# Perceiver block on one core: rows of a context block, its staging and the keys padded to whole 64 bytes

## The chip, the cores and the metric

The kernel runs on one core of one Trainium2 chip. The metric is device time in microseconds (us), the median of several runs. A core has five engines that run side by side: TensorE (PE in the profile; its weight loads are PEld), VectorE (DVE), ScalarE (ACT), GpSimd (POOL) and SyncE (SP), whose queue issues all of this kernel's DMAs. Tiles lie in the on-chip memory SBUF, 128 partitions wide; a tile's row is what one partition holds of it.

## The reference

The input is x, 8 x 64 x 512, and a context of 8 x 1601 x 512. Two layers are computed: cross-attention to the context, a state-space block, a ternary linear map, a second cross-attention, a self-attention and an octonion-structured gated map. Only the first cross-attention touches the change:

```python
q = (query @ Wq + bq).reshape(B, L, NKV, G, HDIM)     # 8 x 64 queries, 32 heads of 128
k_, v_ = jnp.split(kv @ Wkv + bkv, 2, axis=-1)        # 1601 rows of context, 8 key heads
scores = jnp.einsum('blkgd,bmkd->bkglm', q, k) * scale
attn = jax.nn.softmax(scores, axis=-1)
o = jnp.einsum('bkglm,bmkd->blkgd', attn, v).reshape(B, L, NHEAD * HDIM)
return o @ Wo + bo
```

Keys and values have to be worked out for all 1601 rows of each of the 8 batches.

## The kernel before

Accuracy near fp32 is kept by splitting each operand into a high and a low half (type fp32r) and adding three products: high x high, high x low, low x high. The helper `split` (L96) makes the halves: ScalarE writes the high one (L101, or L104 with a bias), and another engine subtracts it from the source for the low one (L102 or L105).

The transposed context of one batch is taken in six blocks of columns, `BLK` (L27): five of 256 and a last one of 322, for 1601 rows padded to 1602. `x_ctx` (L291) loads a block in four pieces of 128 partitions into a staging tile `cst` (three buffers, L300), and splits each into the block's tile, GpSimd writing the low half. Blocks 0 to 4 use `cxb` (five buffers, L298), block 5 uses `cxt` (one buffer, L296). Either holds 2 halves x 4 pieces of rows in a partition; a row of `cxb` has 256 words, one of `cxt` 322, which is 1288 bytes.

Work goes over 64 units, (batch b, key head i), in `x_all` (L501 on). In a unit, six steps s run over the blocks:
- `x_k` (L345) makes the keys of a block: 12 matmuls (4 pieces x 3 products) with the weights wk as the stationary operand and the context as the moving one, into k_ps; then `split` with a bias writes both halves of the tile `kt` (three buffers, L356; rows of 322 words for every block, though five of the six fill 256).
- `x_v` (L310) makes the values of a tile of 128 context rows: 12 matmuls with the context stationary and the weights wv moving, into v_ps. Tiles 10 and 11 (and 12, of 65 rows) come out of `cxt`. It runs once for two heads.
- `x_s` (L360) makes scores: for each 128 keys three matmuls with kt stationary and the queries q moving, into s_ps, which ScalarE copies (L377) and VectorE takes a maximum of (L379, L381).
- softmax (`x_exp`, L405), values (`x_av`, L428) and the output weights (`x_wo`, L470) follow one unit later.

Beside this, generators of the other layers (`chain`, `prep`) are advanced by a planner's costs, so that their work fills gaps; the last group of two batches runs its chain alone in the last tenth of the time. `cxt`, `cxb`, `cst` and `kt` are in one pool, `xp`, whose tiles stand in memory in the order of their first use: S, wk, cxb, cst, kt, wv, q, mx, v, cxt, and then mc, ss, sl, rw, ot, wo. A tile's start is rounded up to 32 bytes.

Of the kernel before, what the change touches and what calls it, by code (L numbers as in the profile page):

```python
# [9 lines left out]
FR = mybir.dt.float32r  # L10
# [6 lines left out]
P = 128  # L17
D = 512
NC = 4
T = 64  # L20
LK = 1601
LP = 1602
NKV = 8
G = 4
NT = 13
# [50 lines left out]
class Kernel:  # L76
# [66 lines left out]
    def consts(self):  # L143
# [12 lines left out]
        def ld(name, shape):  # L156
            t = c.tile(shape, FP, name="c_" + name)
            nc.sync.dma_start(out=t, in_=i[name])
            return t

        self.bq = ld("bq", [P, 32])
        self.bk = ld("bk", [P, NKV])
        self.bv = ld("bv", [P, NKV])

# [24 lines left out]
    def scratch(self):  # L189
# [3 lines left out]
        def t(name, shape):  # L193
            return d.tile(shape, FP, name="d_" + name)

        B = self.B
        self.wk_s = [t(f"wk{k}", [P, 2, NC, P]) for k in range(NKV)]
        self.wv_s = [t(f"wv{k}", [P, 2, NC, 256]) for k in range(NKV // 2)]
        self.q_s = [t(f"q{k}", [B, P, 2, G, T]) for k in range(NKV)]
        self.wo_s = [t(f"wo{k}", [P, G, 2, D]) for k in range(NKV)]  # L200
        self.ot_s = [[t(f"ot{g}_{k}", [P, 1 + (g > 0), G, T]) for k in range(NKV)] for g in range(B // 2)]
# [89 lines left out]
    def x_ctx(self, b, k):  # L291

        nc = self.nc
        o, w = BLK[k]
        if k == 5:
            t = self.sb("cxt", [P, 2, NC, 322], FR, pool=self.xp, bufs=1)  # L296
        else:
            t = self.sb("cxb", [P, 2, NC, 256], FR, pool=self.xp, bufs=5)  # L298
        for c in range(NC):
            st = self.sb("cst", [P, 322], pool=self.xp, bufs=3)  # L300
            nc.sync.dma_start(out=st[:, :w], in_=self.i["ctxT"][b, c, :, o : o + w])
            self.split(t[:, 0, c, :], t[:, 1, c, :], st[:, :w], eng=nc.gpsimd)
        self.ctxb[(b, k)] = t
# [41 lines left out]
    def x_k(self, b, i, blk, w):  # L345

        nc = self.nc
        wd = BLK[blk][1]
        cx = self.cblk(b, blk)
        ps = self.px.tile([P, D], FP, name=self.nm("k_ps"), tag="kv", bufs=KVB)  # L350
        k = 0
        for c in range(NC):
            for a, m in ((0, 0), (0, 1), (1, 0)):
                nc.tensor.matmul(ps[:, :wd], lhsT=w[:, a, c, :], rhs=cx[:, m, c, :], start=k == 0, stop=k == 11)  # L354
                k += 1
        kt = self.sb("kt", [P, 2, 322], FR, pool=self.xp, bufs=3)  # L356
        self.split(kt[:, 0, :wd], kt[:, 1, :wd], ps[:, :wd], bias=self.bk[:, i : i + 1])
        return kt

# [616 lines left out]
    def xattn1(self, bs, x, xo):  # L976
# [7 lines left out]
        def scores(k, b):  # L984
            q0 = k * T
            if self.tail:
                s = self.sb("bc", [T, LP])
                S = [s[:, :512], s[:, 512:1024], s[:, 1024:]]
# [368 lines left out]
def _layout(inp):  # L1357
# [7 lines left out]
    r["ctxN"] = cx  # L1365
    ct = np.zeros((B, D, LP), f)
    ct[:, :, :LK] = np.transpose(cx, (0, 2, 1))
    r["ctxT"] = ct.reshape(B, NC, P, LP)
    r["Wq"] = inp["L0_xattn_Wq"].reshape(NC, P, NKV, D).transpose(2, 1, 0, 3)
# [66 lines left out]
```

## Time and profile before

| | |
|---|---|
| time, median of 3 runs | 2748.9 us (2741.76 to 2750.92) |
| the profiled execution | 2747.45 us, span 2745.6 us |
| TensorE busy | 2584.6 us, 94% of the span, 17840 matmul records |
| VectorE, ScalarE, GpSimd busy | 1756.7, 1378.4, 1163.1 us |
| v_ps matmuls from cxb, from cxt | 3840 (521.5 us), 1152 |
| k_ps matmuls from cxb, from cxt | 3840 (560.9 us), 768 (128.3 us) |
| s_ps matmuls | 2496 (414.9 us) |
| loads into cst | 192 DMAs |

Busy time of a group is the union of its instructions' spans. Matmuls are pipelined: the mean duration of one is longer than its distance to the next, so the distance between starts is worked out from the timeline where it matters. The chain of work that ended last is followed back from the last instruction; its shares say whose time set the end.

### The profile page before, as it was taken

To read this page: it belongs to the slowest core of one execution; us is meant where nothing else is said; L and a number is where in the kernel's file an instruction comes from. 1 tells how busy PE (TensorE), PEld (TensorE's weight loads), DVE (VectorE), ACT (ScalarE), POOL (GpSimd) and SP (SyncE) were. 2 spreads that over 40 slices of the span, in tenths; PEclk is the share of its full clock that TensorE was granted. 3 is DMA by queue.
4 is the path that set the end of the run, shared out by engine and by line. 5 is a ranking of instruction groups with operands and counts; after the bars stand their busy time and mean duration, and the time that the engine had idled before them with its cause. 6 is when DMAs were issued, how large, how long until landed. Compare 5 with 4: busy or idle time off the path is not lost.

```text
span 2745.6 us, 47783 instructions
## 1 busy us (share of the span) xinstructions
PE 2584.6 (94%) x17840; PEld 2303.7 (84%) x17840; DVE 1756.7 (64%) x2988; ACT 1378.4 (50%) x3318; POOL 1163.1 (42%) x1175
## 2 busy tenths in 40 slices
PE   7999999999999899999999989999999999976778
PEld 6999999889889899978988988988897998954545
DVE  4544345577777886545587787454668787549645
ACT  4444555444556554544456555444556555435433
POOL 3212444474579653421367344421348435215220
PEclk9999999999999999999999999999999999978889
DMA  9544446664666234664325534665333543465676
GB/s 305 151 144 152 131 155 221 204 205 156 212 208 212 71 116 164 215 192 155 114 78 156 156 106 131 199 203 165 125 101 97 168 153 126 146 221 197 219 253 218
DMA packets 312167, 460.03 MB, mean 168 GB/s; under 512 B 81272, under 2 KB 188792, under 8 KB 307456
## 3 DMA queue, kind: packets, MB, share of 16 engines
q1 hardware_dynamic: 311936, 456.99, 51.6%
q8 instruction: 140, 2.29, 0.3%
q14 instruction: 91, 0.75, 0.1%
HBM read 384.42 MB, written 72.48 MB: 166 GB/s over the span
## 4 chain that ended last, share of the span: by engine, by line
PE 60%; DVE 15%; DMA 9%; POOL 7%; issue 5%; ACT 4%; SPq 1%; POOLq 0%; DVEq 0%; ACTq 0%
PE v_ps L325 14%; PE k_ps L354 13%; PE o_ps L438 8%; PE s_ps L374 7%; DVE a L62 4%; PE w_ps L495 3%; POOL a L62 3%; PE acc L270 2%; POOL ss L426 2%; PE acc L1000 2%; PE acc L1053 2%; PE acc L740 2%; DMA cst<-in_ctxT_dram 2%; PE acc L743 1%; PE acc L785 1%
## 5 line engine op out<-in xcount | busy, mean ns | idle before, releaser
L354 PE MATMUL k_ps<-cxb,wk 128*128 128x256 f32 x3840 | 560.9, 291 | 21.8 <-ACT cxb L101 9.6
L354 PEld LDWEIGHTS k_ps<-cxb,wk 128*128 128x128 f32 x3840 | 504.9, 191 | 55.8 <-issue 15.1
L325 PE MATMUL v_ps<-wv,cxb 128*128 128x256 f32 x3840 | 521.5, 283 | 7.4 <-DVE mx L381 3.3
L325 PEld LDWEIGHTS v_ps<-wv,cxb 128*128 128x128 f32 x3840 | 479.2, 189 | 28.2 <-issue 13.9
L374 PE MATMUL s_ps<-q,kt 128*128 128x256 f32 (+1 forms) x2496 | 414.9, 299 | 13.3 <-DVE kt L105 4.9
L438 PE MATMUL o_ps<-S,v 128*128 128x256 f32 (+1 forms) x1664 | 409.2, 380 | 1.7 <-ACT S L416 1.6
L374 PEld LDWEIGHTS s_ps<-q,kt 128*128 128x128 f32 (+1 forms) x2496 | 339.7, 185 | 38.0 <-DVE kt L105 7.2
L381 DVE TENSOR_TENSOR mx<-s_ps,mx 128x512 f32<-128x512 f32 x256 | 175.3, 685 | 306.5 <-ACT S L377 306.3
L426 POOL TENSOR_TENSOR ss<-ss,S 128x512 f32<-128x512 f32 x256 | 355.0, 1387 | 16.2 <-ACT S L416 1.5
L377 ACT COPY S<-s_ps 128x512 f32<-128x512 f32 (+1 forms) x448 | 241.5, 551 | 211.8 <-PE s_ps L374 210.7
L438 PEld LDWEIGHTS o_ps<-S,v 128*128 128x128 f32 (+1 forms) x1664 | 296.4, 190 | 33.9 <-ACT S L416 2.5
L418 POOL TENSOR_TENSOR ss<-S,S 128x512 f32<-128x512 f32 x64 | 84.2, 1316 | 566.2 <-ACT S L416 566.0
L104 ACT ACTIVATE kt<-k_ps,c_bk 128x256 fp32r<-128x256 f32 (+1 forms) x384 | 184.7, 481 | 220.1 <-PE k_ps L354 216.1
L105 DVE SCALAR_TENSOR_TENSOR kt<-k_ps,c_bk,kt 128x256 fp32r<-128x256 f32 (+1 forms) x384 | 187.7, 489 | 144.0 <-ACT kt L104 143.2
L415 DVE TENSOR_TENSOR S<-S,m_ps 128x512 f32<-128x512 f32 (+1 forms) x448 | 257.6, 641 | 28.6 <-PE m_ps L401 27.6
L416 ACT ACTIVATE S<-S 128x512 f32<-128x512 f32 (+1 forms) x448 | 247.2, 599 | 42.5 <-DVE S L415 41.9
L328 ACT COPY v<-v_ps 128x256 f32<-128x256 f32 (+1 forms) x416 | 152.3, 367 | 219.6 <-PE v_ps L325 217.9
L62 ACT ACTIVATE a<-lv,c_A_log 128x128 f32<-128x128 f32 x384 | 122.7, 392 | 126.6 <-DVE lv L62 120.3
L62 POOL TENSOR_TENSOR a<-bc,lv 128x512 f32<-128x512 f32 x96 | 128.2, 1336 | 127.7 <-DVE a L62 112.4
L102 POOL TENSOR_TENSOR cxb<-cst,cxb 128x256 fp32r<-128x256 f32 x160 | 126.3, 804 | 120.9 <-ACT cxb L101 118.0
L62 DVE TENSOR_TENSOR_SCAN a<-a,a 128x512 f32<-128x512 f32 x96 | 145.1, 1512 | 48.3 <-POOL a L62 47.9
L325 PE MATMUL v_ps<-wv,cxt 128*128 128x256 f32 (+1 forms) x1152 | 161.8, 286 | 2.2 <-DVE kt L105 2.2
(348 smaller groups left out, 3972.0 us busy)
## 6 DMA issues: line engine op xcount, KB each, us to landing
wo<-d_wo SPq DMA_DIRECT2D x96, 512.0 KB, 4.9
wk<-d_wk SPq DMA_DIRECT2D x63, 512.0 KB, 3.4
wv<-d_wv SPq DMA_DIRECT2D x31, 1024.0 KB, 7.0
cst<-in_ctxT_dram SPq DMA_DIRECT2D x160, 128.0 KB, 3.1
b<-in_ctxN_dram SPq DMA_DIRECT2D x36, 512.0 KB, 4.2
d_q<-q_t SPq DMA_DIRECT2D x32, 512.0 KB, 4.3
q<-d_q SPq DMA_DIRECT2D x64, 256.0 KB, 3.6
d_wo<-b SPq DMA_DIRECT2D x32, 512.0 KB, 2.9
```

What stands on the lines that cost most here:

```text
L62: return lambda *a, **k: self.tc.keep_in_program_order(f(*a, **k))
L104: nc.scalar.activation(hi, src, AF.Identity, bias=bias)
L105: eng.scalar_tensor_tensor(lo, src, bias, hi.bitcast(FP), ALU.add, ALU.subtract)
L325: nc.tensor.matmul(ps[:r], lhsT=cx[:, a, c, o : o + r], rhs=w[:, m, c, :], start=k == 0, stop=k == 11)
L354: nc.tensor.matmul(ps[:, :wd], lhsT=w[:, a, c, :], rhs=cx[:, m, c, :], start=k == 0, stop=k == 11)
L374: nc.tensor.matmul(sp[:r, gi, :], lhsT=kt[:, a, u * P : u * P + r], rhs=q[:, m, :], start=k == 0, stop=k == 2)
L377: nc.scalar.copy(s[:r, :n], sp[:r, :n])
L381: nc.vector.tensor_tensor(mx, sp, S[0] if len(S) == 1 else mx, ALU.max)
L415: nc.vector.tensor_tensor(sv, sv, ps[:r, 1:2].to_broadcast([r, w, 256]), ALU.add)
L416: nc.scalar.activation(sv, sv, AF.Exp, scale=ISC)
L426: nc.gpsimd.tensor_tensor(ss, ss, S[n], ALU.add)
L438: nc.tensor.matmul(ps[:, 0], lhsT=self.v[(b, j, t)][:r, hc : hc + P], rhs=S[t // 2][:r, t % 2], start=t == 0, stop=t == NT - 1)
```

## The change

A constant KW = 336 replaces 322 as the row length of the three tiles, so that a row has 1344 bytes, 21 times 64, instead of 1288. The tile `cxt` is allocated with the longer rows and its first 322 columns are used; of `cst` and `kt` the same columns are used as before. The pool's tiles grow by 448 bytes (cxt), and, with the rounding, 3 x 32 (cst) and 3 x 96 (kt), 832 together.

In the two builds every engine's instructions stand in the same order. Addresses in SBUF (bytes in a partition):

| tile | before | after |
|---|---|---|
| cst | 97536, 98848, 100160 | 97536, 98880, 100224 |
| kt, low half 1288 or 1344 on | 101472, 104064, 106656 | 101568, 104256, 106944 |
| wv | 109248 | 109632 |
| q | 117440, 119488 | 117824, 119872 |
| cxt, row r at r x 1288 or 1344 | 139968 | 140352 |
| wk | 48384, 52480 | the same |
| cxb | 56576 to 89344, 8192 apart | the same |

Lines of the changed kernel stand 2 lower.

```diff
@@ -20,6 +20,8 @@
 LP = 1602
+
+KW = 336
 NKV = 8
@@ -293,11 +295,11 @@
         if k == 5:
-            t = self.sb("cxt", [P, 2, NC, 322], FR, pool=self.xp, bufs=1)
+            t = self.sb("cxt", [P, 2, NC, KW], FR, pool=self.xp, bufs=1)[:, :, :, :w]
         else:
             t = self.sb("cxb", [P, 2, NC, 256], FR, pool=self.xp, bufs=5)
         for c in range(NC):
-            st = self.sb("cst", [P, 322], pool=self.xp, bufs=3)
+            st = self.sb("cst", [P, KW], pool=self.xp, bufs=3)
@@ -353,7 +355,7 @@
-        kt = self.sb("kt", [P, 2, 322], FR, pool=self.xp, bufs=3)
+        kt = self.sb("kt", [P, 2, KW], FR, pool=self.xp, bufs=3)
```

## The prediction

> **What bounds the kernel now.** I read the page from the top: engine totals, slices, chain.
>
> ```profile
> span 2745.6 us, 47783 instructions
> PE 2584.6 (94%) x17840; PEld 2303.7 (84%) x17840; DVE 1756.7 (64%) x2988; ACT 1378.4 (50%) x3318; POOL 1163.1 (42%) x1175
> ...
> PE   7999999999999899999999989999999999976778
> ...
> PE 60%; DVE 15%; DMA 9%; POOL 7%; issue 5%; ACT 4%; SPq 1%; POOLq 0%; DVEq 0%; ACTq 0%
> PE v_ps L325 14%; PE k_ps L354 13%; PE o_ps L438 8%; PE s_ps L374 7%; DVE a L62 4%; PE w_ps L495 3%; POOL a L62 3%; PE acc L270 2%; POOL ss L426 2%; PE acc L1000 2%; PE acc L1053 2%; PE acc L740 2%; DMA cst<-in_ctxT_dram 2%; PE acc L743 1%; PE acc L785 1%
> ```
>
> TensorE (PE) is the resource: busy nearly throughout until the last tenth, and 60% of the chain that ended last is its work. Cross-attention's three products (v_ps, k_ps, s_ps) are 34% of the chain, and the padded tiles are operands of some of them. The last tenth uses none of those tiles.
>
> The groups of instructions, shapes kept apart, give their sizes (count, then busy us and mean ns):
>
> ```profile
> L354 PE MATMUL k_ps<-cxb,wk 128*128 128x256 f32 x3840 | 560.9, 291 | 21.8 <-ACT cxb L101 9.6 <-DVE mx L381 8.6 <-ACT S L377 2.4
> L325 PE MATMUL v_ps<-wv,cxb 128*128 128x256 f32 x3840 | 521.5, 283 | 7.4 <-DVE mx L381 3.3 <-ACT v L328 2.8 <-DVE kt L105 0.9
> L374 PE MATMUL s_ps<-q,kt 128*128 128x256 f32 x2304 | 389.4, 300 | 11.8 <-DVE mx L381 3.9 <-DVE kt L105 3.4 <-ACT v L328 2.4
> L354 PE MATMUL k_ps<-cxt,wk 128*128 128x322 f32 x768 | 128.3, 312 | 2.8 <-DVE mx L381 2.6 <-DVE kt L105 0.2
> L325 PE MATMUL v_ps<-wv,cxt 128*128 128x256 f32 x768 | 108.4, 287 | 0.0
> ```
>
> The mean of one is latency, since matmuls overlap. What counts is the distance between starts. The timeline of TensorE shows whole groups of twelve (start, length):
>
> ```profile
> 1002.06 1.59 PE L354 MATMUL k_ps<-cxb,wk 128*128 128x256 f32 x12
> ...
> 1011.21 1.60 PE L325 MATMUL v_ps<-wv,cxt 128*128 128x256 f32 x12
> ...
> 1013.36 1.93 PE L354 MATMUL k_ps<-cxt,wk 128*128 128x322 f32 x12
> ...
> 1032.14 1.54 PE L325 MATMUL v_ps<-wv,cxb 128*128 128x256 f32 x12
> ```
>
> The last line is the fast kind: with 0.28 us for the last matmul itself, (1.54-0.28)/11 = 115 ns per step, against (1.60-0.28)/11 = 120.
>
> **Start distances by operand.** I took the distance between starts of successive matmuls inside one group over the whole trace, leaving out distances over 170 ns (waits). Means: v_ps from cxb (in aligned rows) 115.5 ns, median 114; v_ps from cxt (rows 1288 bytes apart) 118.4, median 118; s_ps from kt 117.9; k_ps from cxt (322 columns) 148.2; k_ps from cxb 119.0, median 120.
>
> [...] the spread of 114 to 120 ns at equal shape shows that something about the operands matters all the same.
>
> **The change, part by part.** No instruction is added or removed. In the two builds each engine's instructions stand in the same order with the same waits, SP's DMA issues included; columns read and written are the same 322. What moves is addresses.
>
> (1) Rows inside cxt. Before, row r of 8 starts 8r bytes past a multiple of 64; after, all start at 0. These are the stationary operands of 1152 v_ps matmuls (768 of full width, 384 of 65 columns). If they reach the distance of the aligned v_ps: 118.4 - 114.4 = 4 ns; 1152 x 4 = 4.6 us.
>
> (2) kt. Its three buffers start at 32, 0, 32 past a multiple of 64, and the low half 1288 bytes on at 40, 8, 40; after, all at 0. 2496 s_ps matmuls: 117.9 - 114 = 3.9 ns; 9.7 us.
>
> (3) k_ps from cxt, the moving operand: 768. [...] But of the eight rows the one that starts at 0 is no faster (148.8 into it, 148.0 to 150 for others), and the 322 columns stay. [...] I take 0.
>
> Sum 14.3 us of TensorE time. How much reaches the end? By the chain, v_ps carries 14% of 2745.6 = 384 us of its 683 us busy, a share of 0.56; s_ps 192 of 415, 0.46. That gives 2.6 + 4.5 = 7 us. By occupation, TensorE is busy 97% of 100 to 2450 us, so at most 14. I take 9, near the lower end, since s_ps is followed by waits of ACT and VectorE (S waits 210.7 us for s_ps).
>
> (4) ScalarE and VectorE at kt and cxt: nothing. Within before, kt's high half takes a median 473 ns into the buffer at 0 and 473 into those at 32; VectorE's low half 475 at offset 8 and 475 at 40. cxt's casts are 461 ns at offsets 0, 8, 16, 24 alike.
>
> (5) GpSimd's low half of cxt: median 755 to 761 ns for the rows 8 bytes off a 16-byte line, 881 to 889 for the two on one. If all four behave like the latter: 2 rows x 8 batches x 125 ns = 2 us more. Covered: in the last batch the tile is done at 2114.4 us and first read at 2129.9. Without the cover, 2 us.
>
> (6) Loads into cst (192 DMAs on SP's queue): buffer starts were 0 or 32 past 64, now 0. First landings of the 256-column loads take a median 1.87 us at 0 and 1.93 at 32: nothing, and ScalarE's wait for them (97 us in all) stays.
>
> (7) Everything behind in the pool shifts: wv, q, mx, v and cxt by 384 bytes, ss, sl, rw, ot, wo by 832. cxb and wk, in front, stay. Multiples of 64, so no start within 64 changes, but wv against cxb goes from 192 to 64 modulo 256. Bounds: the best group of all, v_ps from cxb (3840), could fall to k_ps's 120 (6 ns, 21 us) or keep 114. I take zero.
>
> 2747.45 us (the profiled execution; 1.85 around its span) minus 9 is 2738.5. The median of runs, 2748.9, lies 1.45 above the profiled one: 2740.
>
> **Rivals.** *Alignment sets nothing* (same): k_ps from cxb has every operand on 64 bytes and still steps at 120 ns, slower than misaligned cxt. Something else then gives v_ps from cxb its 114, for instance which tiles lie near each other: wv and cxb lie far apart, while wv and cxt, q and kt, cxb and wk are pairs of neighbours; k_ps from cxt (far apart) looks good for its length. The change leaves those places as they are. Against it: nothing in the trace excludes it. Time 2749, within 4.
>
> *wv meets cxb* (slower): the moved wv collides with the unmoved cxb as wk does (distance 0 modulo 256 there). 3840 x 5.5 = 21 us, times 0.56 = 12: 2761, or 2754 if (1) and (2) come at the same time. It decides from 8.2 / 0.56 / 3840 = 3.8 ns per matmul. For it: distances of 114 and 120 at equally aligned operands. Against: no group with distance 64 is known to be bad (s_ps from the kt buffer at 64 steps at 117.5, between the two).
>
> *All of it at full worth* (faster): [...] 2730.
>
> **How the numbers follow.** Forecast's gain 0.35, full worth 0.05, nothing 0.36, collision 0.24. A measurement of this kernel tells about 0.3% (8.2 us) from no change: its three runs span 9.2 us. Faster 0.40, same 0.36, slower 0.24. The likeliest case's own range is 2732 to 2741, only just beyond that bound; with the others on both sides the range is 2730 to 2761, which leaves the best case's far end and a full collision's far end outside.
>
> **What would show it.** Right: v_ps from cxt in twelve at 1.54 us instead of 1.60, mean latency 283 instead of 287, s_ps under 300, the line of v_ps from cxb unchanged. Wrong: cxt and kt steps still at 118 (nothing), or v_ps from cxb at 1.59 and over 283 ns (collision). GpSimd's cxt line should rise from 899 towards 960 ns and move nothing. A faster total with unchanged steps would mean that my step is wrong, not only its size.

## The result, and the profile after

The changed kernel takes a median of 2754.7 us in 22 runs (2744.88 to 2760.96), the kernel before 2749.8 us in 22 runs beside it (2740.93 to 2756.35). The ratio is 1.0019, with a 95% interval of 1.0011 to 1.0027: about 5 us longer, where 9 us less were forecast. So it moved the other way; it lies inside the forecast range of 2730 to 2761 because that range was drawn wide enough to take in the rivals.

The profiled execution of the changed kernel took 2744.88 us and happens to be the shortest of its 22 runs. Its span can't be set against the span of before; what can be compared is the time from the start of one matmul to the start of the next, here called its step. First its page: totals, the slices of TensorE, and the chain that ended last.

```profile
span 2742.9 us, 47783 instructions
PE 2583.1 (94%) x17840; PEld 2304.4 (84%) x17840; DVE 1757.9 (64%) x2988; ACT 1380.6 (50%) x3318; POOL 1166.4 (43%) x1175
...
PE   7999999999999899999999999999999999976877
...
PE 63%; DVE 14%; DMA 7%; POOL 7%; ACT 4%; issue 4%; SPq 0%; POOLq 0%; DVEq 0%; ACTq 0%
PE v_ps L327 15%; PE k_ps L356 14%; PE o_ps L440 8%; PE s_ps L376 7%; DVE a L64 5%; PE w_ps L497 3%; POOL a L64 3%; PE acc L272 3%; PE acc L1002 2%; DMA cst<-in_ctxT_dram 2%; PE acc L1055 2%; PE acc L742 2%; POOL ss L428 2%; PE acc L787 2%; PE acc L745 1%
```

The picture is that of before: the same engine bounds the same nine tenths. The total of TensorE shows no loss, 2583.1 us against 2584.6. The granted clock was 0.982 in this execution and 0.978 in that of before; 0.4% of 2584 is 10 us, more than is looked for: if busy time goes with the clock, which is an estimate that no run here tests, it could hide the difference. So a total of one execution can't carry the verdict, and the next view is the groups of instructions, shapes kept apart (count, then busy us and mean ns of one, then idle time before them and what ended it).

```profile
L356 PE MATMUL k_ps<-cxb,wk 128*128 128x256 f32 x3840 | 560.8, 291 | 23.0 <-ACT cxb L103 9.5 <-DVE mx L383 9.5 <-POOL cxb L104 1.6
L327 PE MATMUL v_ps<-wv,cxb 128*128 128x256 f32 x3840 | 526.8, 284 | 6.5 <-ACT v L330 2.8 <-DVE mx L383 2.7 <-DVE kt L107 0.9
...
L376 PE MATMUL s_ps<-q,kt 128*128 128x256 f32 x2304 | 388.6, 300 | 12.0 <-DVE kt L107 3.8 <-DVE mx L383 3.8 <-DMA q<-d_q 2.2
...
L356 PE MATMUL k_ps<-cxt,wk 128*128 128x322 f32 x768 | 128.7, 313 | 4.4 <-DVE mx L383 2.7 <-DVE kt L107 1.7
...
L327 PE MATMUL v_ps<-wv,cxt 128*128 128x256 f32 x768 | 106.2, 283 | 0.9 <-ACT v L330 0.9
...
L104 POOL TENSOR_TENSOR cxt<-cst,cxt 128x322 fp32r<-128x322 f32 x32 | 30.2, 949 | 24.5 <-ACT cxt L103 21.9 <-DMA cst<-in_ctxT_dram 2.3
```

One group got clearly worse, and it is one whose operands were not padded: v_ps from cxb, 521.5 us busy before and 526.8 now. The first line, k_ps from cxb, is a control: neither of its operands moved, and it stands at 560.8 against 560.9. v_ps from cxt gained 2.2 us (108.4 to 106.2), s_ps 0.8. The timeline of TensorE shows the same in groups of twelve (start, length, both in us):

```profile
1008.69 1.56 PE L327 MATMUL v_ps<-wv,cxt 128*128 128x256 f32 x12
1010.79 1.96 PE L356 MATMUL k_ps<-cxt,wk 128*128 128x322 f32 x12
...
1016.42 1.59 PE L356 MATMUL k_ps<-cxb,wk 128*128 128x256 f32 x12
...
1029.64 1.57 PE L327 MATMUL v_ps<-wv,cxb 128*128 128x256 f32 x12
```

Twelve v_ps from cxb took 1.54 us before and take 1.57; twelve from cxt took 1.60 and take 1.56. Over the whole trace, worked out as in the prediction (inside a group, steps over 170 ns left out), the mean steps in ns are:

| matmuls | count | before | after | times count |
|---|---|---|---|---|
| v_ps from cxb | 3840 | 115.5 | 117.7 | +8.4 us |
| v_ps from cxt | 1152 | 118.4 | 117.2 | -1.4 us |
| s_ps from kt, 256 columns | 2304 | 118.0 | 118.5 | +1.2 us |
| k_ps from cxt | 768 | 148.2 | 148.9 | +0.5 us |
| k_ps from cxb (control) | 3840 | 119.0 | 119.1 | |

The sum is 8.7 us of TensorE time. With the prediction's share of 0.56 that reaches the end, 4.9 us or 0.18%; measured were 0.19%. Busy times put the sum lower (5.3 - 2.2 - 0.8 + 0.4 = 2.7 us), and they wander: two executions below with the same steps differ by 3 us in one group. So the size is good to a factor of two; that the loss is v_ps from cxb had to be tested. The matmuls o_ps, one of whose operands (v) moved by 384 bytes as well, step at 216.2 ns in both kernels.

### The profile page after: what moved, and what is told of

It reads as the page before. It is cut to its first block, busy times and chain, and to the rows that moved or that the text cites. A ratio compares the mean times of both kernels' runs of the same rounds, so it can differ in the third digit from the quotient of the medians.

```text
span 2742.9 us, 47783 instructions
## 1 busy us (share of the span) xinstructions
PE 2583.1 (94%) x17840; PEld 2304.4 (84%) x17840; DVE 1757.9 (64%) x2988; ACT 1380.6 (50%) x3318; POOL 1166.4 (43%) x1175
## 4 chain that ended last, share of the span: by engine, by line
PE 63%; DVE 14%; DMA 7%; POOL 7%; ACT 4%; issue 4%; SPq 0%; POOLq 0%; DVEq 0%; ACTq 0%
PE v_ps L327 15%; PE k_ps L356 14%; PE o_ps L440 8%; PE s_ps L376 7%; DVE a L64 5%; PE w_ps L497 3%; POOL a L64 3%; PE acc L272 3%; PE acc L1002 2%; DMA cst<-in_ctxT_dram 2%; PE acc L1055 2%; PE acc L742 2%; POOL ss L428 2%; PE acc L787 2%; PE acc L745 1%
## 5 line engine op out<-in xcount | busy, mean ns | idle before, releaser
L356 PE MATMUL k_ps<-cxb,wk 128*128 128x256 f32 x3840 | 560.8, 291 | 23.0 <-ACT cxb L103 9.5
L327 PE MATMUL v_ps<-wv,cxb 128*128 128x256 f32 x3840 | 526.8, 284 | 6.5 <-ACT v L330 2.8
L379 ACT COPY S<-s_ps 128x512 f32<-128x512 f32 (+1 forms) x448 | 241.7, 551 | 212.7 <-PE s_ps L376 211.1
L64 POOL TENSOR_TENSOR a<-bc,lv 128x512 f32<-128x512 f32 x96 | 128.4, 1337 | 129.9 <-DVE a L64 114.3
L104 POOL TENSOR_TENSOR cxb<-cst,cxb 128x256 fp32r<-128x256 f32 x160 | 125.9, 802 | 121.4 <-ACT cxb L103 118.2
```

Source lines behind the costliest of these rows:

```text
L64: return lambda *a, **k: self.tc.keep_in_program_order(f(*a, **k))
L327: nc.tensor.matmul(ps[:r], lhsT=cx[:, a, c, o : o + r], rhs=w[:, m, c, :], start=k == 0, stop=k == 11)
L379: nc.scalar.copy(s[:r, :n], sp[:r, :n])
```

## Experiments

The theory: what sets the step is the distance from the start of the stationary operand to the start of the moving one, modulo 256 bytes (distance is used below for these bytes alone). In wv, cxb and wk all rows are multiples of 256 bytes long, so all of v_ps from cxb has one distance (192 before, 64 after), and so has all of k_ps from cxb (0 in both). The rivals: alignment of the padded rows does something after all and costs elsewhere; or the change in time is chance. A third rival stays open throughout: that the place of each operand counts by itself, and not the distance. By the order of the tiles cxb starts at a multiple of 256 in every kernel below, so v_ps from cxb is changed through its moving operand alone and k_ps from cxb through its stationary one, and no run moves both operands of a group together.

Only addresses move in these kernels: a tile gets a few words more and its contents start a few words on. Unless said otherwise each starts from the kernel before.

**Shift without padding.** wv 384 bytes on, as the change moves it; rows stay at 1288 bytes.

```diff
+    def wv_tile(self):
+        t = self.sb("wv", [P, 2144], FR, pool=self.xp, bufs=1)
+        return t[:, 96 : 96 + 2048].rearrange("p (a c k) -> p a c k", a=2, c=NC)
-            w = self.sb("wv", [P, 2, NC, 256], FR, pool=self.xp, bufs=1)
+            w = self.wv_tile()
```

> Rows stay at 1288 bytes; wv begins 384 bytes later inside its tile, and q, mx, v and cxt behind it move by 384 as they do in the change. Theory (the distance of wv from cxb sets the step of v_ps from cxb): the step goes from a mean of 115.5 ns to 117.7 as in the changed kernel, v_ps from cxt stays near 118.4, and the time is 0.15 to 0.35% over before (8.4 us of TensorE time, about 0.56 of it on the chain, is 4.7 us). Rival (the padded rows themselves make it slower): v_ps from cxb at 115.5 and a ratio of 1.000 within 0.001.

Measured: 1.0016 of before (1.0007 to 1.0024). In its groups of instructions:

```profile
L329 PE MATMUL v_ps<-wv,cxb 128*128 128x256 f32 x3840 | 527.7, 284 | 7.3 <-DVE mx L385 3.3 <-ACT v L332 2.8 <-DVE kt L105 0.9
```

527.7 us and a step of 117.7 ns: the changed kernel's values without any padded row. The shift of wv and of what lies behind it makes the loss; padded rows aren't needed for it.

**Padding with wv put back.** The changed kernel, with wv another 128 bytes on, which brings the distance back to 192.

```diff
+        t = self.sb("wv", [P, 2080], FR, pool=self.xp, bufs=1)
+        return t[:, 32 : 32 + 2048].rearrange("p (a c k) -> p a c k", a=2, c=NC)
```

> The changed kernel with wv 128 bytes further on, so that it lies again at 192 modulo 512 as before the change (cxb at 256), and q, mx, v and cxt with it. Theory: v_ps from cxb returns to 115.5 ns, v_ps from cxt keeps what the padding gave it (117.2) or better, the time is 0.998 to 1.000 of before. Rival (padded rows are what costs): v_ps from cxb returns perhaps, but the ratio stays at 1.002.

Measured: 1.0006 (0.9996 to 1.0017). Groups first, then the timeline of TensorE:

```profile
L331 PE MATMUL v_ps<-wv,cxb 128*128 128x256 f32 x3840 | 521.4, 283 | 6.3 <-DVE mx L387 3.2 <-ACT v L334 1.7 <-DVE kt L107 0.9
```

```profile
1009.09 1.57 PE L331 MATMUL v_ps<-wv,cxt 128*128 128x256 f32 x12
...
1016.84 1.59 PE L360 MATMUL k_ps<-cxb,wk 128*128 128x256 f32 x12
...
1030.04 1.54 PE L331 MATMUL v_ps<-wv,cxb 128*128 128x256 f32 x12
```

The twelve are at 1.54 us again, the step at 115.7 ns, the busy time at 521.4 us. With all rows padded, the kernel can't be told from before: the padded rows themselves bring nothing that the time shows. The time alone doesn't tell this kernel from the shift without padding either, since their intervals overlap; the steps do.

**wk moved.** If the distance rules, then k_ps from cxb, at distance 0 with steps of 119.0 ns, must get faster when wk is moved so that its distance is 192.

```diff
+    def wk_tile(self):
+        t = self.sb("wk", [P, 1152], FR, pool=self.xp, bufs=2)
+        return t[:, 16 : 16 + 1024].rearrange("p (a c k) -> p a c k", a=2, c=NC)
-        w = self.sb("wk", [P, 2, NC, P], FR, pool=self.xp, bufs=2)
+        w = self.wk_tile()
```

> Rows stay at 1288 bytes; wk begins 64 bytes later inside a larger tile, so that the moving cxb stands to the stationary wk as wv stands to cxb in the kernel before (448 modulo 512); all other distances modulo 512 stay. Theory (distance modulo 512 or 256 sets the step): k_ps from cxb goes from a mean of 119.0 ns to about 115.5, 3840 x 3.5 = 13 us of TensorE time, about half on the chain: ratio 0.996 to 0.998. Rival (which tiles are neighbours, or which is moving, sets it): k_ps stays at 119 and the ratio is 1.000 within 0.001.

Measured: 0.9972 (0.9962 to 0.9981). Groups, then timeline:

```profile
L358 PE MATMUL k_ps<-cxb,wk 128*128 128x256 f32 x3840 | 554.9, 290 | 20.9 <-ACT cxb L101 9.4 <-DVE mx L385 7.9 <-ACT S L381 1.9
L329 PE MATMUL v_ps<-wv,cxb 128*128 128x256 f32 x3840 | 522.9, 284 | 8.2 <-DVE mx L385 3.1 <-ACT v L332 2.9 <-DMA wv<-d_wv 1.3
```

```profile
1022.23 1.54 PE L358 MATMUL k_ps<-cxb,wk 128*128 128x256 f32 x12
...
1029.85 1.55 PE L329 MATMUL v_ps<-wv,cxb 128*128 128x256 f32 x12
```

Twelve k_ps from cxb, at 1.59 us before and after the change, now take 1.54, and the step is 116.5 ns, where 115.5 was expected. Every operand of this group lay on whole 64 bytes before and does now; what changed is the place of wk and with it the distance.

One thing here the theory doesn't explain. v_ps from cxb kept its distance of 192, and yet its step rose from 115.5 to 116.2 ns; v_ps from cxt at full width, neither of whose operands moved against the other, fell from 118.8 to 117.8. Two more executions with wk moved and rows unpadded repeat both (116.2 and 116.1; 117.8 and 117.7). So the distance of a group's own operands isn't all that sets its step; the rest, up to 1 ns, is open.

**wv at distance 0.** The other way round: v_ps from cxb is put where k_ps was.

```diff
+        t = self.sb("wv", [P, 2048 + 128], FR, pool=self.xp, bufs=1)
+        return t[:, 16 : 16 + 2048].rearrange("p (a c k) -> p a c k", a=2, c=NC)
```

> wv begins 64 bytes later inside a tile made 512 bytes larger: distance to cxb 0 modulo 512, like cxb to wk in k_ps. Theory: v_ps from cxb steps at about 119 to 120 ns, as k_ps does. Rival (only far moves matter, or neighbourhood): 115.5.

> The kernel with wv 64 bytes on (distance to cxb 0 modulo 256), now timed. v_ps from cxb steps at 119.6 ns, 4.1 over before: 3840 x 4.1 = 15.7 us of TensorE time. Theory (about 0.56 of it reaches the end): 8.8 us, ratio 1.0025 to 1.004. Rival (v_ps has slack, the steps are only a sign of something else): ratio under 1.0015, no more than for the distance of 64.

The first is one execution (2758.05 us), read by its steps: 119.6 ns. The second is the same kernel timed: 1.0030 (1.0021 to 1.0038). Its groups and its timeline:

```profile
L358 PE MATMUL k_ps<-cxb,wk 128*128 128x256 f32 x3840 | 562.2, 291 | 22.9 <-ACT cxb L101 10.2 <-DVE mx L385 8.9 <-ACT S L381 2.1
L329 PE MATMUL v_ps<-wv,cxb 128*128 128x256 f32 x3840 | 534.1, 287 | 7.5 <-ACT v L332 3.1 <-DVE mx L385 3.0 <-DVE kt L105 0.9
```

```profile
1025.83 1.59 PE L358 MATMUL k_ps<-cxb,wk 128*128 128x256 f32 x12
...
1033.53 1.60 PE L329 MATMUL v_ps<-wv,cxb 128*128 128x256 f32 x12
```

This is the full collision, which the prediction had priced at 5.5 ns and which measures 4.1: 1.60 us for twelve, 287 ns, 534.1 us busy. The sum agrees in size: 4.1 ns x 3840 = 15.7 us, times 0.56 = 8.8 us, 0.32%, and 0.30% were measured.

**The other distances.** Four kernels, one execution each, move wv and wk together by different amounts: tiles of 2176 and 1152 words, the contents starting 48, 64, 80, 8 words on in wv and 8, 32, 64, 4 in wk.

```diff
+        t = self.sb("wv", [P, 2176], FR, pool=self.xp, bufs=1)
+        return t[:, 48 : 48 + 2048].rearrange("p (a c k) -> p a c k", a=2, c=NC)
+        t = self.sb("wk", [P, 1152], FR, pool=self.xp, bufs=2)
+        return t[:, 8 : 8 + 1024].rearrange("p (a c k) -> p a c k", a=2, c=NC)
```

> Rows of 1288 bytes; distance (moving minus stationary, modulo 512) of wv to cxb 128 and of cxb to wk 480. Theory with 448 as the one good place and 256 as the period: both steps at 117 to 119 ns. Rival (anything but 0 is as good as any other): v_ps from cxb 115.5 and k_ps from cxb 116.5.

> Distance of wv to cxb 192, of cxb to wk 384, modulo 512. If the period is 256, wv at 192 is the same as 448: v_ps from cxb 115.5; if it is 512 or more, 117 to 118. k_ps at 384 (128 modulo 256): 117 to 118.5.

> Distance 256 modulo 512 for both. If the period is 256, both step as at 0: 119 to 120 ns. If it is 512 or more, something else, 117 or less.

> Distance of wv to cxb 480 (32 bytes before), of cxb to wk 496 (16 before), modulo 512. If the step follows the distance smoothly: v_ps from cxb between 115.5 and 119.6, near 117.5; k_ps from cxb near 118.5. If only whole 64 bytes count, 480 and 496 behave like 448 (115.5 and 116.5) or like 0 (119.6 and 119).

Their times (2756.14, 2752.28, 2758.49, 2755.10 us, with one run of before at 2746.51) order among themselves as the steps of the two groups do, but that of before doesn't fit (115.5 and 119.0 ns, against 115.4 and 118.5 at 2752.28 us), and one run each settles nothing. The steps can be compared; mean ns:

| distance modulo 256 | v_ps from cxb | k_ps from cxb |
|---|---|---|
| 192 | 115.5 (before, 448), 115.7 (wv put back), 115.4 (192), 116.2 (wk moved) | 116.5 (wk moved) |
| 64 | 117.7 (after), 117.7 (shift alone) | |
| 224 | 118.2 (480) | 118.2 (480) |
| 240 | | 118.3 (496) |
| 128 | 118.8 | 118.5 (384) |
| 0 | 119.6 (wv at 0), 119.6 (256) | 119.0 (before), 118.9 (256) |

In brackets stands the kernel, the distance modulo 512, or both. The two columns, one changed through its moving and one through its stationary operand, agree within 1.0 ns and have the same order, which speaks for the distance against the place of each operand by itself, but doesn't settle it. A distance and the same plus 256 give the same step (115.5 ns at 448 and 115.4 at 192; 119.6 at 0 and at 256): these distances fit a period of 256 bytes, and not half of it, which would make 64 and 192 alike, which stand at 117.7 and 115.5. Distances of 224 and 240 (118.2 and 118.3 ns), at which starts are not whole 64 bytes apart, are no worse than 128 and 0 (118.5 to 119.6), at which they are.

The place in the group says a little more. In v_ps from cxb, means over groups of twelve that stand alone, the first steps are alike (118.7 ns before, 120.1 after), and from the fifth on they settle: at 114.3 to 114.7 before, at 117.2 to 117.9 after, at 119.8 to 120.0 with the distance 0. k_ps from cxb settles at 115.3 to 116.0 with wk moved.

**Only the rows of cxt padded**, kt and cst as before:

```diff
-            t = self.sb("cxt", [P, 2, NC, 322], FR, pool=self.xp, bufs=1)
+            t = self.sb("cxt", [P, 2, NC, 336], FR, pool=self.xp, bufs=1)[:, :, :, :w]
```

> Only the rows of cxt padded to 1344 bytes; cst, kt and all that lies before cxt stay where they were, and only mc, ss, sl, rw, ot and wo behind it move. Theory: v_ps from cxt 118.4 to about 117.5, GpSimd's low half of cxt slower (949 ns), nothing else: ratio 0.999 to 1.000. Rival (padding has a cost of its own, as the second run's 1.0006 might say): 1.0005 or more.

Measured: 0.9995 (0.9983 to 1.0006). v_ps from cxt steps at 117.8 ns (full width) and 117.4, against 118.8 and 117.8 before: a gain of some 0.8 ns in the mean, where the prediction had 4. 0.8 ns x 1152 is 0.9 us, below what a time shows. Moving wk, with no row padded, had brought v_ps from cxt at full width to the same 117.8.

**Padding with both distances at 192.** The changed kernel, wv 128 bytes on and wk 64 bytes on (a tile of 1088 words), in two sessions:

```diff
+        t = self.sb("wv", [P, 2080], FR, pool=self.xp, bufs=1)
+        return t[:, 32 : 32 + 2048].rearrange("p (a c k) -> p a c k", a=2, c=NC)
+        t = self.sb("wk", [P, 1088], FR, pool=self.xp, bufs=2)
+        return t[:, 16 : 16 + 1024].rearrange("p (a c k) -> p a c k", a=2, c=NC)
```

> The changed kernel with both wk and wv put at the good distance (192 modulo 256). Theory: k_ps from cxb 116.5, v_ps from cxb 115.7 to 116.2, and the same time as the kernel with wk alone moved: ratio 0.996 to 0.998. Rival (padded rows cost of their own): 0.998 or more.

> The eleventh run again. If padding costs: 0.998 to 1.000, above e12 and e14 by 0.001 or more. If the difference was chance: 0.997 to 0.998, the same as they.

Measured: 0.9990 (0.9981 to 0.9998) and 0.9988 (0.9979 to 0.9996). The steps are 116.0 and 116.2 ns (v_ps and k_ps from cxb), in the second 115.9 and 116.3. That was less than wk alone had brought (0.9972), and less than the 0.996 to 0.998 expected, which left open whether padding costs something here. Three more kernels were timed beside the second of these: wk moved in the kernel before with the smaller tile, the same with kt and cst padded too (and wv put back to 192) but not cxt, and the first wk kernel again. The edit of the first of them:

```diff
+        t = self.sb("wk", [P, 1088], FR, pool=self.xp, bufs=2)
+        return t[:, 16 : 16 + 1024].rearrange("p (a c k) -> p a c k", a=2, c=NC)
```

> No padded rows; wk 64 bytes on in a tile 256 bytes larger (512 in the third run), so that only the larger layout differs from the third run. If padding costs time: 0.9972 again (0.996 to 0.998). If the placement made the difference: 0.999.

> As the twelfth run, with the rows of kt and cst padded, wv put back to its distance of 192, and cxt unpadded. If kt's padding costs: 0.999; if cxt's does or none: 0.997.

> The third run again (wk 64 bytes on in the larger tile, rows unpadded): 0.9972, between 0.996 and 0.998.

Measured: 0.9982 (0.9972 to 0.9991), 0.9980 (0.9971 to 0.9990) and 0.9986 (0.9977 to 0.9994). The first wk kernel went from 0.9972 to 0.9986 by being timed again, so the difference that raised the question is no more than one kernel's ratio varied between two sessions, 0.14%. The groups of the small wk tile:

```profile
L358 PE MATMUL k_ps<-cxb,wk 128*128 128x256 f32 x3840 | 551.8, 288 | 23.2 <-ACT cxb L101 10.5 <-DVE mx L385 8.6 <-POOL cxb L102 1.7
L329 PE MATMUL v_ps<-wv,cxb 128*128 128x256 f32 x3840 | 522.0, 283 | 7.7 <-ACT v L332 3.4 <-DVE mx L385 3.1 <-DVE kt L105 0.9
```

551.8 us here and 554.9 in the larger tile, with steps of 116.5 ns in both: this is the scatter of a busy time.

Moving wk 64 bytes beats the kernel before: six measurements between 0.9972 and 0.9990, every interval below 1. Padded rows or not makes no difference that they show.

## Why the prediction was wrong

Of 14.3 us of TensorE time to be gained, in steps (1) and (2), 0.2 came in all; 8.4 us were lost in step (7), which was set to zero.

**Step (7), the shift of what lies behind, taken as zero: failed.** It named the right pair, the right distances (192 to 64 modulo 256) and bounds of 0 to 21 us, and then took the lower end. The runs put 2.2 ns on each of 3840 matmuls, 8.4 us of TensorE time and some 4.7 at the end. The argument against was that no group at distance 64 was known to be bad; but none with a single distance of 64 was known at all, and in the kernel before the only two groups with one distance each stood at 115.5 (192) and 119.0 (0). That was a hint that the distance matters, and then 192, the better place seen, had more to lose than to gain. The upper bound has a slip: 6 ns x 3840 is 23 us, and 21 belongs to 5.5 ns. The rival *wv meets cxb* is what happened, at 2.2 ns instead of 5.5: below the 3.8 ns that it would have taken to be seen as slower by 0.3%.

**Step (1), cxt rows, 4 ns: failed in size.** 1.2 ns in the changed kernel, 0.7 with wv put back, 0.8 with these rows alone; and with wk moved there is none (117.8 ns at full width in the unpadded kernel, 117.9 in the padded). It rested on the aligned v_ps being 4 ns faster because it is aligned. It is faster with wv at 192, as wv at distance 0 shows: all aligned, and 119.6 ns. The 4 ns were also too many for that comparison, here and in step (2): a mean of 118.4 was set against 114.4, close to the median of v_ps from cxb (114), where its mean was 115.5. Mean against mean, the two steps come to 3.3 and 6.0 us instead of 4.6 and 9.7. That the padded rows still gain a little is not explained by any run: their distances to wv are 0, 192, 128 and 64 in turn, and the steps into their matmuls in the changed kernel, 118.6, 116.7, 117.1 and 117.0 ns in the mean, don't follow the table above (119.6, 115.5, 118.8, 117.7).

**Step (2), kt, 3.9 ns and 9.7 us: failed.** s_ps went from 118.0 to 118.5 ns, and stayed within 117.7 to 118.9 in every kernel. The wait of ScalarE for s_ps is 211.1 us in all, 210.7 before. The largest term of the sum came to nothing. Each of these kernels mixes several distances between q and kt, so that a gain by alignment, cancelled by distances, isn't excluded.

**Step (3), k_ps from cxt, taken as 0: right.** 148.2 and 148.9 ns. That it could be worth more, as the lower end of the range (2730) has it, was the author's estimate; no run shows it.

**Steps (4) and (6): right as far as seen.** VectorE's low half of kt is 476 ns in the mean and ScalarE's high half 471, against 477 and 471 before. ScalarE and GpSimd waited 101.5 us for the loads into cst, 97.3 before; with the shift alone, where cst is as before, it is 101.6, so padding isn't needed for that.

**Step (5), GpSimd: right.** All rows of cxt now take a median of 878 to 893 ns, as the two rows that start at a multiple of 16 bytes had done (881 to 889; the prediction says on a 16-byte line and means no more than this), and the mean of the line rose from 899 to 949, with 960 forecast. Before, its line was:

```profile
L102 POOL TENSOR_TENSOR cxt<-cst,cxt 128x322 fp32r<-128x322 f32 x32 | 28.6, 899 | 25.4 <-ACT cxt L101 25.0
```

It is covered as said: the last tile is done at 2115.8 us and first read at 2132.7.

**The share that reaches the end, 0.56: not contradicted.** The changed kernel (8.7 us, about 5.2 measured) and wv at 0 (15.7 us, 8.2) agree with it; neither is measured sharply enough to show it. The total was wrong through its terms, not through this factor.

The rival *alignment sets nothing* came nearest in its cause: it looked for it in where tiles lie, and its key observation was k_ps from cxb at 120 ns with every operand on 64 bytes. But it named nearness, and a move of 64 bytes, which leaves near tiles near, took k_ps from 119.0 to 116.5 ns. It also went wrong in its last sentence, that the change leaves those places as they are. Both rivals together, little gain from alignment and a small collision, give the result.

For the stationary rows of cxt, 1288 bytes apart instead of 1344 cost 0 to 1.7 ns at full width: 118.8 ns before and 117.1 after the change, 117.8 and 117.9 with wk moved in both. The 4 ns that the prediction had estimated did not come. For these fp32r matmuls of 256 columns the place of the moving operand, with the stationary one where it was, changes the step by up to 4.1 ns (v_ps from cxb, 115.5 before and 119.6 with wv at distance 0); by what mechanism no run here shows.

Open: why the steps fit a period of 256 bytes; whether the distance or the place of each operand counts, which a kernel with both operands of a group moved together would tell; why v_ps moved with wk; and which rule sets s_ps and v_ps from cxt, whose rows mix several distances.

## What to carry to other kernels

A change of a tile's size moves every tile behind it in the pool, and in this kernel, whose TensorE is busy 94% of the span, the shift weighed more than the change itself (by the steps, 8.4 us of TensorE time against 0.2): work out the distances between moving and stationary operands, before and after. Where two groups of equal shape step differently and alignment is the same, move one of them by 64 bytes and look; here it was worth 0.1 to 0.3% for one line. Experiments that only move addresses, one tile at a time, separate such causes well, and the steps in one trace tell them apart where the total time can't.

## What the hardware showed that was not expected

The step of these fp32r matmuls of 128 x 128 by 256 columns changed in these runs with the place of an operand modulo 256 bytes, and fits the distance of the two operands' starts: in v_ps from cxb 115.5 ns at 192, 117.7 at 64, 118.2 at 224, 118.8 at 128 and 119.6 at 0. It isn't symmetric (64 and 192 differ by 2.2 ns). Starts on whole 64 bytes are not enough for a short step (119.6 at 0), and starts off them (118.2 at 224) were no worse than that. The distance is not all of it: the same group at 192 took 116.2 ns when wk alone was moved.

GpSimd wrote the low half of 322 columns (medians) in 755 to 761 ns in rows of cxt that start 8 bytes past a multiple of 16 (before), and in 878 to 893 ns when all rows start at one (after): the aligned rows are the slower ones, by some 125 ns. With only the rows of cxt padded the mean is 950 ns, where the changed kernel has 949. Here that is hidden: the last tile is done 16.9 us before it is first read.
